# Norm products of q behind the tenth dense matmul, and the next batch's rows six positions apart

## Chip, cores and metric

The kernel runs on one core of one Trainium2 chip. Its time is the device time of that core in microseconds (us), from timed runs without a profiler; beside them stands one execution taken by the hardware profiler, whose records all views of the profile come from.

## What is computed

x is (4, 512, 512) in f32: four batches of 512 tokens, 512 wide. Three blocks follow one another, each on a layernorm of x:

```python
x = x + 0.5 * ffn(layernorm(x))
x = x + attention(layernorm(x))
x = x + 0.5 * ffn(layernorm(x))
```

The ffn is `down(silu(gate(x)) * up(x))` with 2048 inner columns; its weights are interpolated from control points. The attention, which is the stage of the change, is a gated delta rule with 16 key heads and 32 value heads of 128 columns (two value heads share one key head):

```python
q, k, v, z = split(x @ W_qkvz)                  # by key head
q, k, v = silu(causal_conv_of_4_taps(q, k, v))  # along the tokens
q = inv_scale**2 * rms_norm(q);  k = inv_scale * rms_norm(k)
beta = sigmoid(b);  g = -exp(A_log) * softplus(a + dt_bias)   # a, b from x @ W_ba
for each token t and value head:
    S = S * exp(g_t)
    delta = (v_t - k_t @ S) * beta_t
    S = S + outer(k_t, delta)
    o_t = q_t @ S
out = (rms_norm(o) * norm_w * silu(z)) @ W_out
```

## The kernel before

The tokens of a batch are cut into four chunks of 128, and the recurrence over tokens is done chunk by chunk as matmuls (f32), with the inverse of a triangular matrix for the part inside a chunk. The attention walks through 64 units, 4 batches of 16 key heads, in slots: `slot(un)` (L1533) holds the work of unit `un` and, beside it, that of its neighbours.

Of unit `un` itself: the projections of q and of the two v, each of four dense matmuls (`project`, L1033; the matmul is L1041, 128x128 weights against 512 columns, in the profile `pj` with w_q, w_v, w_k). Behind the fourth matmul of each come, by a calendar, the convolution (`taps`: one ScalarE step at L1049, three VectorE steps at L1051, all called acc), three positions later tanh on ScalarE (th, L1059) and one position later the silu on VectorE (L1063), which gives q or v. Of unit `un`+8 (`LEAD` is 8): the projection of its key (w_k), again four dense matmuls. Then 16 more dense matmuls: the gates z of this and the next unit in even slots (pz, L1359), the output projection of two finished units in odd ones (py, L1507). These 32 matmuls are the list `dense`.

Of unit `un`-1: the recurrence, eleven steps from `recur` (L1390) for its four chunks. `read_state` multiplies k and q with the state (pks, L1398), then VectorE makes rr (L1408) and, one position later, ScalarE tq (L1415). `solve` multiplies rr with the inverse (pzz, L1423), which ScalarE copies to zz (L1425). `write_state` multiplies zz with ks and pT (pos, L1434 and L1436), whence VectorE makes the new state (L1441, L1445) and, one position later, oo (L1451, L1455). Of unit `un`-2: the gating and turning of its outputs (`scale_outputs` L1485; `turn_o` with pgt, L1490, and gT, L1492).

The order is written out by hand. A slot goes through positions i = 0, 1, 2 and so on. At each it first does what the calendar has due (`later(d, f)` puts f d positions on), then the steps listed for this position by `after(i, step)`, then dense matmul i, so that position i lies behind i dense matmuls. The steps of the recurrence are put at the front of positions 1, 3, 5, 8, 10, 12, 16, 18, 20, 23 and 26: solve of the second chunk is at 8, its write_state at 10, read_state of the third at 12, its solve at 16. The instructions of TensorE, VectorE, ScalarE and GpSimd run in the order in which this code issues them; that of the DMAs on SyncE's queue is left to the compiler.

`norm` (L1244) is one of the steps of `after`. It takes the squared norms of q for the scaling of the RMS norm: `products` (L1067, the matmuls at L1072) does 16 small matmuls of 32x32 into a PSUM tile pqq; one position later `mean_square` (L1074) takes the diagonal on VectorE (dg, L1077), reduces and scales it (msq, L1079 and L1080) and has GpSimd take the root (rsq, L1082); three positions after that `roots` (L1254) makes rq and rqe, which the recurrence of this unit uses in the next slot. `norm` stands at position 9, together with `diagonal`, which works on the matrix to be inverted. `turn_k` (L1231; transposes of k, then ks on GpSimd) and `scores` (L1275; products k·k and k·q, pp) stand at 11 and 13. PSUM tiles come from three pools: pa with four banks (pj, pqq, py, pz, pp, pgt, pk, ln_pt and others share them in turn), pq and pi with two each.

Ten slots before a batch begins, in the slots un = 6, 22 and 38 (the "batch slots" for short), the rows of that batch are fetched and normalized by `begin` (L918), for t = 0 to 3: `load(t)` (L924) starts the DMA of 128 rows (L926) into xt, a tile with two buffers which it shares with osq, sp and et; three positions later `stats` (L931 to L936) takes mean and variance on VectorE and the root on GpSimd; one position later VectorE scales the rows (L938); `turn(t)` (L940), in the code of the slot `turn_x`, transposes them on TensorE into ln_pt (L945) and ScalarE copies that to xnT (L946). `load(t)` stands at position 7t and `turn_x(t)` at 7t + 6. In the slot that follows, the gates beta and g of the new batch are made (`log1p`, L979 to L998, on VectorE). Once a slot GpSimd multiplies out ee (`decay`, L1221), which has 1024 elements in each of 128 partitions.

Of the kernel before, what the change touches and what calls it, by code (L numbers as in the profile page):

```python
# [264 lines left out]
def tile_macaron(ctx, tc, x, w_qkvz, w_ba, conv_w, dt_bias, a_log, norm_w, w_out, cps, consts, grid, starts, out):  # L265
# [555 lines left out]
    def attention():  # L821


        with ExitStack() as st:
# [76 lines left out]
            def due():  # L901
                for f in calendar.pop(clock[0], ()):
                    f()
# [578 lines left out]
            def scale_outputs(s, r):  # L1482
                for t in range(NT):
                    u = 2 * t + r
                    nc.scalar.activation(s["oo"][:, t, r], s["oo"][:, t, r], AF.Copy, scale=s["orr"][:, u : u + 1])  # L1485

            def turn_o(s, r):
                po = bank(pa, "pgt", [P, NT, P])
                for t in range(NT):
                    nc.tensor.transpose(po[:, t, :], s["oo"][:, t, r, :], ident)  # L1490
                gr = w4.tile([P, NT, P], F32, name="gT")
                nc.scalar.activation(gr, po, AF.Copy, scale=nwh)  # L1492
                s["pair"].setdefault("gT", []).append(gr)

            def load_o(pair, n):
                pair["wo"] = w1.tile([P, 4, H], F32, name="w_o")
                nc.sync.dma_start(
                    pair["wo"], w_out[(n - 1) * 2 * DK : (n + 1) * 2 * DK, :].rearrange("(r p) h -> p r h", p=P)
                )

            def project_out(pair, xa):
                box = {}

                def step(t, r):
                    if r == 0:
                        box["py"] = bank(pa, "py", [P, H])
                    nc.tensor.matmul(box["py"], pair["gT"][r][:, t, :], pair["wo"][:, r, :], start=r == 0, stop=r == 3)  # L1507
                    if r == 3:
                        py = box["py"]
                        later(1, lambda: nc.vector.tensor_tensor(xa[:, t, :], py, xa[:, t, :], ALU.add))  # L1510

                return [lambda t=t, r=r: step(t, r) for t in range(NT) for r in range(4)]
# [7 lines left out]
            def keys_of(un):  # L1520
                b, n = units[un]

                def dd():
                    if un % GRP == 0:
                        diag[un // GRP] = w1.tile([P, 8 * GRP, BLK], F32, name="dd")
                    return diag[un // GRP]

                return keys(b, n, batches[b], heads[un], dd, un % GRP)
# [4 lines left out]
            def slot(un):  # L1533


                dense, at = [], {}

                def after(i, *steps):
                    at.setdefault(i, []).extend(steps)

                if un < N:
                    b, n = units[un]
                    pair = pairs.setdefault((b, n // 2), {})
                    p = prepare(un, b, n, batches[b], heads[un], inverse[un // GRP], un % GRP, pair)
                    if un == 0:
                        p["load"]()
                        p["load_z"]()
                        p["decay"]()
                        p["scan"]()
                    dense += p["dense"]  # L1550
                    after(11, p["turn_k"])
                    after(9, p["norm"], p["diagonal"])
                    after(11, lambda: p["scores"](0))
                    after(13, lambda: p["scores"](1))
                    after(17, p["join32_a"])
                    after(20, p["join32_b"])
                    after(21, lambda: p["turn_v"](0))
                    after(22, lambda: p["turn_v"](1))
                    after(23, lambda: p["join64"](0, None))
                    after(26, lambda: p["join64"](1, 0))  # L1560
                    after(29, lambda: p["join64"](None, 1))
                ku = un + LEAD
                if ku < N:
                    kk = keys_of(ku)
                    kk["load"]()
                    kk["decay"]()
                    dense += kk["dense"]
                    after(24, kk["blocks"])
                if un < N and n % 2 == 0:
                    dense += p["gates"]  # L1570
                if un >= 3 and units[un - 2][1] % 2:
                    b2, n2 = units[un - 2]
                    pair2 = pairs[b2, n2 // 2]
                    if n2 == 1:
                        xas[b2] = w1.tile([P, NT, H], F32, name="xa")
                        nc.sync.dma_start(xas[b2], x1[b2].rearrange("(t p) h -> p t h", p=P))
                    load_o(pair2, n2)
                    dense += project_out(pair2, xas[b2])
                if 2 <= un < N + 2:
                    last = un >= N  # L1580
                    after(0 if last else 2, lambda: scale_outputs(heads[un - 2], 0))
                    after(0 if last else 4, lambda: scale_outputs(heads[un - 2], 1))
                    after(0 if last else 6, lambda: turn_o(heads[un - 2], 0))
                    after(0 if last else 8, lambda: turn_o(heads[un - 2], 1))
                if 1 <= un < N + 1:
                    steps = recur(heads[un - 1], units[un - 1][1])
                    for i, f in zip((1, 3, 5, 8, 10, 12, 16, 18, 20, 23, 26), steps):
                        at.setdefault(i, []).insert(0, f)
                    after(22, lambda: square_sums(heads[un - 1], 0))
                    after(28, lambda: square_sums(heads[un - 1], 1))  # L1590
                    after(30, lambda: gate_outputs(heads[un - 1]))

                turn = un % GRP
                if turn == 0 and un + GRP < N:
                    running["inv"] = invert(diag[un // GRP + 1], inverse[un // GRP + 1])
                inv = running.get("inv") if un < N else None

                if un + LEAD + 2 < N and units[un + LEAD + 2][1] == 0:
                    b1 = units[un + LEAD + 2][0]
                    running["begin"] = begin(b1)  # L1600
                    batches[b1], load, turn_x, raw, sums = running["begin"]
                    for t in range(NT):
                        after(7 * t, lambda t=t: load(t))
                        after(7 * t + 6, lambda t=t: turn_x(t))
                if un + LEAD + 1 < N and units[un + LEAD + 1][1] == 0:
                    _, _, _, raw, sums = running["begin"]
                    after(3, raw)
                    after(24, sums)
                if un + 1 < N:
                    b1, n1 = units[un + 1]  # L1610

                    def loads():
                        q = prepare(un + 1, b1, n1, batches[b1], heads[un + 1], None, 0, pairs.setdefault((b1, n1 // 2), {}))
                        q["load"]()

                    after(13, loads)
                    for i, f in ((17, "decay"), (27, "scan")):
                        after(i, lambda f=f: prepare(un + 1, b1, n1, batches[b1], heads[un + 1], None, 0, pairs[b1, n1 // 2])[f]())
                    if n1 % 2 == 0:
                        after(31, lambda: prepare(un + 1, b1, n1, batches[b1], heads[un + 1], None, 0, pairs[b1, n1 // 2])["load_z"]())  # L1620
                for i in range(max(len(dense), max(at, default=0) + 1)):
                    due()
                    for f in at.get(i, ()):
                        f()
                    if i < len(dense):
                        dense[i]()
                    if inv is not None and i in PUMP:
                        next(inv, None)
                    clock[0] += 1
                if inv is not None and turn == GRP - 1:  # L1630
                    for _ in inv:
                        pass
                if un >= N:
                    drain()
                if 2 <= un < N + 2:
                    b2, n2 = units[un - 2]
                    if n2 == NK - 1:
                        due()
                        nc.sync.dma_start(x2[b2].rearrange("(t p) h -> p t h", p=P), xas[b2])
# [108 lines left out]
```

## Time and profile before

| what | value |
| --- | --- |
| timed runs, us | 3836.11, 3828.24, 3830.8; median 3830.8 |
| the profiled execution, its own time, us | 3776.52 |
| its span, first to last instruction, us | 3774.6 |
| granted TensorE clock, mean over the span (1.00 is full speed) | 0.974 |
| the 64 slots of the attention, roughly | 560 to 3340 us |
| busy in that stretch, us: TensorE | 2722.9 of 2780 |
| VectorE | 2156.8 |
| ScalarE | 1222.8 |
| GpSimd | 670.5 |
| share of the 16 DMA engines there | 0.21, 64 GB/s |
| granted TensorE clock there | 1.00 |

How to read it. PE is TensorE, PEld its loading of weights (which runs beside the matmuls), DVE VectorE, ACT ScalarE, POOL GpSimd, SP SyncE. L1041 is line 1041 of the kernel, `pj<-xnT,w_v` says which tiles an instruction writes and reads, x4 how many instructions a row gathers. In a timeline a row has its start (us from the start of the span), the time that the group took, engine, line and tile; in brackets stands how long the engine was idle before it and whose end it then waited for. The chain of work goes back from the last instruction of a window to what released each step; "issue" there is time in which nothing that the profile shows was waited for. In a table by windows each row has the window, its length, the busy time (and number of instructions) of PE, PEld, DVE, ACT and POOL, then the granted clock, the share of the DMA engines and their GB/s. The ends of matmuls are modelled in the records, so a busy TensorE need not be one at its peak. Before and behind the 64 slots lie the two ffn blocks and the start of the attention, which the change does not touch.

### The profile page before, as it was taken

What the parts mean: (1) busy time and instruction counts of PE and PEld (TensorE: products, weight loads), DVE (VectorE), ACT (ScalarE), POOL (GpSimd) and SP (SyncE); (2) the same over time, 40 slices, a digit from 0 to 9 for tenths busy, and PEclk for the clock granted to TensorE, in tenths of its full rate; (3) what the DMA queues carried; (4) which work ended last, traced back from release to release, by engine and by line L of the source; (5) the groups of instructions that cost most, each with busy time, mean ns of one, the idle gap of its engine ahead of it and who ended that gap; (6) DMA issues with size and microseconds to landing.
All of it is one profiled execution on the core that took longest, in us unless ns stands there. A gap on an engine that the chain in (4) does not pass through costs nothing.

```text
span 3774.6 us, 62529 instructions
## 1 busy us (share of the span) xinstructions
PE 3561.9 (94%) x24568; PEld 1967.6 (52%) x24568; DVE 2544.4 (67%) x5928; ACT 1471.3 (39%) x3440; POOL 867.2 (23%) x655
## 2 busy tenths in 40 slices
PE   5999679999999999999999999999999999987998
PEld 2333245555555555555555555555555555553333
DVE  5223687777777787777777777777778777552321
ACT  2322134444444444444444444444444444442221
POOL 2113112212222222222222222222222221210221
PEclk7999889999999999999999999999999999997999
DMA  4436311212222222122122222222221111203452
GB/s 140 158 129 189 107 46 53 69 56 64 65 73 59 82 65 73 53 65 63 60 59 82 60 71 61 60 65 69 66 82 60 63 51 51 70 18 109 152 199 90
DMA packets 303093, 302.25 MB, mean 80 GB/s; under 512 B 96880, under 2 KB 231312, under 8 KB 302224
## 3 DMA queue, kind: packets, MB, share of 16 engines
q1 hardware_dynamic: 292560, 264.70, 22.4%
q0 software_dynamic: 10240, 33.56, 2.9%
q8 instruction: 194, 3.18, 0.3%
q14 instruction: 99, 0.81, 0.1%
HBM read 247.60 MB, written 50.59 MB: 79 GB/s over the span
## 4 chain that ended last, share of the span: by engine, by line
PE 68%; DVE 15%; POOL 6%; ACT 5%; DMA 3%; issue 3%; SPq 0%; DVEq 0%; POOLq 0%; ACTq 0%
PE pj L1041 14%; PE py L1507 11%; PE pz L1359 9%; DVE acc L1051 4%; PE pks L1398 4%; PE y L492 3%; PE pp L1283 3%; PE pg L439 3%; PE pu L439 3%; POOL oo L1480 3%; PE pos L1436 2%; DVE ee L1227 2%; PE pu L1344 2%; PE pzz L1423 2%; POOL orr L1479 2%
## 5 line engine op out<-in xcount | busy, mean ns | idle before, releaser
L1051 DVE SCALAR_TENSOR_TENSOR acc<-pj,cw,acc 128x511 f32<-128x511 f32 (+2 forms) x768 | 574.6, 748 | 187.4 <-ACT acc L1049 169.2
L1041 PE MATMUL pj<-xnT,w_v 128*128 128x512 f32 x1024 | 520.6, 601 | 0.0
L1359 PE MATMUL pz<-w_z,xnT 128*128 128x512 f32 x1024 | 514.0, 614 | 0.0
L1507 PE MATMUL py<-w_o,gT 128*128 128x512 f32 x1024 | 511.0, 613 | 0.4
L448 DVE TENSOR_TENSOR ffn_it<-pu,ffn_sg 128x512 f32<-128x512 f32 x128 | 88.4, 691 | 364.8 <-PE pu L439 251.4
L1041 PE MATMUL pj<-xnT,w_q 128*128 128x512 f32 x512 | 256.5, 604 | 9.4 <-ACT ksq L1112 9.4
L1041 PE MATMUL pj<-xnT,w_k 128*128 128x512 f32 x512 | 246.3, 601 | 3.4 <-DVE acc L1051 3.2
L1415 ACT ACTIVATE tq<-pks,rqe 128x128 f32<-128x128 f32 x384 | 120.3, 364 | 330.7 <-DVE rq L1256 192.6
L1485 ACT ACTIVATE oo<-oo,orr 128x128 f32<-128x128 f32 x512 | 162.7, 390 | 206.2 <-POOL oo L1480 206.2
L1082 POOL TENSOR_TENSOR rsk<-msk,phalf 128x4 f32<-128x4 f32 x64 | 66.9, 1045 | 719.2 <-DVE msk L1080 712.1
L1049 ACT ACTIVATE acc<-pj,cw 128x512 f32<-128x512 f32 x256 | 175.3, 685 | 137.4 <-PE pj L1041 137.4
L1507 PEld LDWEIGHTS py<-w_o,gT 128*128 128x128 f32 x1024 | 170.8, 190 | 108.5 <-issue 97.4
L1359 PEld LDWEIGHTS pz<-w_z,xnT 128*128 128x128 f32 x1024 | 170.2, 191 | 101.4 <-issue 90.4
L1082 POOL TENSOR_TENSOR rsq<-msq,phalf 128x4 f32<-128x4 f32 x64 | 65.0, 1015 | 681.8 <-DVE msq L1080 669.1
L1059 ACT ACTIVATE th<-acc 128x512 f32<-128x512 f32 x256 | 161.7, 632 | 147.7 <-DVE acc L1051 143.6
L1041 PEld LDWEIGHTS pj<-xnT,w_v 128*128 128x128 f32 x1024 | 170.5, 191 | 71.0 <-issue 64.4
L1221 POOL TENSOR_TENSOR ee<-ident,w 128x1024 f32<-128x1024 f32 x64 | 141.4, 2209 | 225.6 <-DVE pT L1292 225.6
L458 POOL DMA_INDIRECT nat<-hid,idx x128 | 123.2, 963 | 300.1 <-PE y_pt L509 104.1
L1473 DVE TENSOR_REDUCE om<-osq 128x4 f32<-128x512 f32 x128 | 87.1, 681 | 154.1 <-ACT osq L1472 154.1
L1166 DVE TENSOR_TENSOR inv<-inv,inv_tmp 128x30 f32<-128x30 f32 (+14 forms) x480 | 169.1, 352 | 16.5
L1479 POOL TENSOR_TENSOR orr<-om,phalf 128x8 f32<-128x8 f32 x64 | 105.1, 1642 | 311.9 <-DVE om L1477 311.9
L1423 PEld LDWEIGHTS pzz<-rr,tt 128*128 128x128 f32 x768 | 115.0, 193 | 114.8 <-DVE rr L1408 49.5
(213 smaller groups left out, 6836.5 us busy)
## 6 DMA issues: line engine op xcount, KB each, us to landing
hid<-ffn_it SPq DMA_DIRECT2D x128, 256.0 KB, 2.1
w_v<-in_L_attn_W_qkvz SPq DMA_DIRECT2D x64, 512.0 KB, 3.5
w_z<-in_L_attn_W_qkvz SPq DMA_DIRECT2D x64, 512.0 KB, 4.7
ab<-decay_c SPq DMA_DIRECT2D x64, 512.0 KB, 3.6
w_o<-in_L_attn_W_out SPq DMA_DIRECT2D x32, 1024.0 KB, 5.5
w_k<-in_L_attn_W_qkvz SPq DMA_DIRECT2D x64, 256.0 KB, 2.8
w_q<-in_L_attn_W_qkvz SPq DMA_DIRECT2D x64, 256.0 KB, 3.3
ad<-decay_b SPq DMA_DIRECT2D x256, 32.0 KB, 2.3
```

The costliest lines, as they stand in the source:

```text
L439: nc.tensor.matmul(pm, wc[k // 2][:, m, at : at + P], ft[k // 2], start=True, stop=True)
L1041: nc.tensor.matmul(pj, w()[:, c, col : col + DK], xnT[:, c, :], start=c == 0, stop=c == NC - 1)
L1049: nc.scalar.activation(acc, pj, AF.Copy, scale=cw[:, ch, 3:4])
L1051: nc.vector.scalar_tensor_tensor(acc[:, d:], pj[:, : S - d], cw[:, ch, 3 - d : 4 - d], acc[:, d:], ALU.mult, ALU.add)
L1059: nc.scalar.activation(th, box["acc"], AF.Tanh)
L1166: nc.vector.tensor_tensor(ee[:, j + 1 :, :j], ee[:, j + 1 :, :j], tj, ALU.add)
L1359: nc.tensor.matmul(pz, xnT[:, c, t * P : (t + 1) * P], pair["wz"][:, c].rearrange("p j k -> p (j k)"), start=c == 0, stop=c == NC - 1,)
L1398: nc.tensor.matmul(pks[:, j].rearrange("p r v -> p (r v)"), m[:, tok], box["state"].rearrange("p r v -> p (r v)"), start=True, stop=True,)
L1423: nc.tensor.matmul(pzz[:, r], s["tT"][:, 2 * t + r], rr[:, r], start=True, stop=True)
L1479: nc.gpsimd.tensor_tensor(s["orr"], om, phalf, ALU.pow)
L1485: nc.scalar.activation(s["oo"][:, t, r], s["oo"][:, t, r], AF.Copy, scale=s["orr"][:, u : u + 1])
L1507: nc.tensor.matmul(box["py"], pair["gT"][r][:, t, :], pair["wo"][:, r, :], start=r == 0, stop=r == 3)
```

## The change

Two edits in `slot`. The squared norms of q are taken at position 10 and no longer at 9, which puts them behind the tenth dense matmul, and behind the step of the recurrence at that position, since those are put in front. `diagonal` stays at 9. All that `norm` puts on the calendar moves on by one position with it: dg, the reduction and GpSimd's root from 10 to 11, rq and rqe from 13 to 14. In the three batch slots the rows are loaded at positions 0, 6, 12, 18 in place of 0, 7, 14, 21 and turned at 5, 11, 17, 23 in place of 6, 13, 20, 27; statistics and scaling follow the loads, at 3, 9, 15, 21 and 4, 10, 16, 22. Nothing is added to the work or taken from it.

```diff
@@ in slot(un) @@
                     after(11, p["turn_k"])
-                    after(9, p["norm"], p["diagonal"])
+                    after(9, p["diagonal"])
+                    after(10, p["norm"])
                     after(11, lambda: p["scores"](0))
...
                     for t in range(NT):
-                        after(7 * t, lambda t=t: load(t))
-                        after(7 * t + 6, lambda t=t: turn_x(t))
+                        after(6 * t, lambda t=t: load(t))
+                        after(6 * t + 5, lambda t=t: turn_x(t))
```

From this edit on every line of the changed kernel has a number higher by one.

## The prediction

> **What bounds the kernel now.** I read the page first, then who waits for whom on TensorE in the attention stage, then the chain of work through one slot, then the timeline of that place, and last the granted clock where a batch changes.
>
> From the page:
>
> ```profile
> span 3774.6 us, 62529 instructions
> PE 3561.9 (94%) x24568; PEld 1967.6 (52%) x24568; DVE 2544.4 (67%) x5928; ACT 1471.3 (39%) x3440; POOL 867.2 (23%) x655
> ```
>
> TensorE is the bound, and a gain must come out of the time in which it does nothing. The waits of TensorE alone in 560 to 3340 us, which is nearly all of the 64 slots (us in total, times, longest):
>
> ```profile
> PE pqq L1072 <- DVE q L1063: 35.1, 47, 0.8
> PE pks L1398 <- DVE state L1441: 10.0, 6, 3.3
> PE pzz L1423 <- DVE rr L1408: 8.0, 10, 1.1
> ```
>
> The first is the step that is moved; the second belongs almost wholly to the three slots that load the next batch (3.06, 3.07 and 3.35 us). The chain of work in 1130 to 1139.5 us, an ordinary slot:
>
> ```profile
> 1132.23 1.73 PE pj L1041 x4
> 1133.96 0.04 issue
> 1134.00 0.63 ACT tq L1415 x2
> 1134.63 0.58 ACT gT L1492
> 1135.21 0.53 ACT th L1059
> 1135.73 0.02 issue
> 1135.76 0.70 DVE q L1063
> 1136.46 0.04 issue
> 1136.51 0.46 PE pqq L1072 x32
> ```
>
> For 2.5 us the path leaves TensorE: ScalarE works through its queue (tq, gT, th), VectorE makes q, and pqq starts 0.05 us after that. The timeline of TensorE there, and below the dots the same place two slots later:
>
> ```profile
> 1134.72 1.02 PE L1041 MATMUL pj<-xnT,w_v 128*128 128x512 f32 x2
> 1136.51 0.46 PE L1072 MATMUL pqq<-q 128*32 128x32 f32 x32 [0.76 <-DVE q L1063]
> 1136.89 1.13 PE L1041 MATMUL pj<-xnT,w_v 128*128 128x512 f32 x2
> 1137.86 0.61 PE L1434 MATMUL pos<-zz,ks 128*128 128x128 f32 x4
> ...
> 1224.89 1.02 PE L1041 MATMUL pj<-xnT,w_v 128*128 128x512 f32 x2
> 1225.93 0.46 PE L1072 MATMUL pqq<-q 128*32 128x32 f32 x32
> 1226.31 1.12 PE L1041 MATMUL pj<-xnT,w_v 128*128 128x512 f32 x2
> 1227.28 0.61 PE L1434 MATMUL pos<-zz,ks 128*128 128x128 f32 x4
> ```
>
> From pj to pos it is 3.14 us in the upper slot and 2.39 in the lower, where q came in time. Of 64 slots 45 have the wait of 0.76 us, three (the batch slots) 0.60, the first one 12.2, and 15 none.
>
> **Part one: norm one matmul later.** A dense matmul is two passes of 0.43 us, 0.86 together. In the upper slot the ninth ends at 1134.72 + 0.86 = 1135.58. After the change the tenth follows at once, to 1136.44. Next is no longer pqq: at position 10 the recurrence's write_state stands first, then norm. Its pos products (four short ones with ks, four with pT, 0.44 + 0.45 us) need zz, which ScalarE copies from 1136.18 to 1136.57, behind the same tq, gT, th and one acc. So the wait is not gone but changes its cause: zz can be used at about 1136.62, 0.18 us late. Weights that are loaded only at the release cost a little more: a pzz group that had to wait took 0.58 us to its successor (816.71 to 817.29), an unhindered one 0.44 (1224.01 to 1224.46 in the lower slot), so +0.14. The pos group ends near 1136.62 + 0.89 + 0.14 = 1137.65. Then pqq: changing to its narrow weights cost 0.17 us in the lower slot (1224.89 + 0.86 to 1225.93), its products 0.38, and the dense matmul behind them runs 0.10 longer (1.13 against 1.02). The eleventh dense matmul in effect starts at 1138.30. Before, it started at 1138.75. The gain is 0.45 us, 0.53 if the change of weights behind the short pos products is half as dear; I take 0.5.
>
> What could take it back further on in the slot? Behind pqq VectorE runs without idling from q on (1135.76), and the sum of its work is unchanged, only reordered: state and oo now come ahead of dg, the reduction and the scaling (0.28 + 0.29 + 0.17, about 0.7 us with their gaps). So the new state is ready 0.7 us earlier and the next pks has more room than its 1.16 us. rr of position 12 comes at the same time as before, 1145.55; its reader pzz stood at 1146.99 with weights wanted 0.43 earlier, so about 0.5 us remain after the shift. The third pks started 0.84 us after its state, where one that waits starts 0.145 after: 0.7 us of room, plus 0.39 that VectorE idled on TensorE before (acc at 1102.85) and gets back. None is used up by 0.5, though little is left. POOL's rsq and ks come about 0.9 us later; ks is read in the next slot, and roots, moved from position 13 to 14 with norm, finds rsq done. One wait is new. In the built program the first key matmul (position 12; past the last key head a gate or output matmul) takes over pqq's PSUM bank, and waits for dg. dg ends near 1140.5 and that matmul would start at about 1142.2: 1.5 us of room.
>
> The slots: 45 of the 0.76 kind, of which three follow a batch slot. There VectorE also makes the gates (L979 to L998) and TensorE already waits for rr at 830.61 and for state at 836.66, so what is gained at pqq is lost there. 42 x 0.5 = 21. The 15 slots without a wait gain about 0.1 (a switch to narrow weights in a better place): 1.5. In the first slot one dense matmul moves under the 12.2 us: 0.9.
>
> **Part two: rows every six positions.** Twelve loads, statistics, scalings and turns move, in three slots of 64. No work is added, and from load to statistics (three positions) and on to the scaling nothing changes; only the turn comes one position sooner after it. On SP's queue two row loads now stand ahead of w_v, which is used a slot later (issued at 768.60): nothing. The buffer of row t is that of row t-2, whose turn (6t-7) is ahead of the load at 6t. Row 0: scaled by 756.37, turned at 756.88 or later: no wait. Its copy by ScalarE (0.60 us at 761.21) leaves the place ahead of th, so q is 0.5 earlier in that slot. Row 1: its scaling ends at about 767.1, the turn would come at 766.6: 0.5 us of wait, in which state comes anyway. Row 3 falls where VectorE idles 4.4 us: nothing. Row 2 decides. Before, its scaling (780.17) ran into POOL's ee (779.90) and took 1.92 us, not 0.55; that pushed state, and pks waited 3.06 us. After, VectorE's statistics end near 775.5, POOL's root near 776.1, and ee starts at once behind it, so the scaling meets it again: done at 778.1, while TensorE wants the turn at 775.2 to 775.8. The wait moves from pks to the turn, about 2.5 us, and state (taps 2.31, ww 0.86, state 0.60 later) arrives at 781.8, when pks does too. Saved are about 0.6 us of wait and the turn's 0.44, already done: 1 us a slot.
>
> [...] The trace, window by window (the column ahead of the last two is the granted clock):
>
> ```profile
> 780.00:784.00 4.00, 1.15 (x3) 1.00 (x4) 3.94 (x8) 0.42 (x1) 1.80 (x1) 0.78 0.00 0
> 784.00:790.00 6.00, 6.00 (x63) 3.65 (x62) 3.01 (x9) 2.83 (x8) 0.00 (x0) 0.58 0.00 0
> ```
>
> So each batch slot also loses about 3 us at half clock (782.2 to 789.0). [...] I go by the row: the clock halves again, 1 us a slot, 3 in all. [...]
>
> **Sum.** 21 + 1.5 + 0.9 + 3 = 26.4 us. Against the profiled execution, 3776.5 us: 3750. The median of the timed runs, 3830.8, is 54 us above it, and no view shows where. If TensorE is slower there by that 1.4%, the 18 us from the previous slot's last pos product to pqq stretch by 0.25: the 0.76 becomes 0.51 and the wait for zz vanishes, so the gain per slot is still 0.5. Predicted median: 3830.8 - 26 = 3805.
>
> **Rivals.** (a) As worked out, 3805: 0.56. (b) More: zz holds nobody (its copy or the weight load is dearer in my sum than on the chip), so the whole 0.76 goes: 45 x 0.76 = 34, with the rest 39, 3792; or the batch slots keep full clock, 9 more, 3796. For it: waits of TensorE on zz are nearly absent now (0.3 us). Against: ScalarE's queue times leave no doubt that zz comes after 1136.44. 0.2. (c) VectorE sets the pitch: the 0.5 us of room behind pzz and pks is smaller than it looks, TensorE waits there, and some 8 us remain: 3823. For it: VectorE never idles from q to the key taps. Against: slots without the wait pass pzz and pks freely, 44.5 us long instead of 45.1. 0.19. (d) Slower: the key matmul waits for dg, which now stands behind state and oo. It decides once dg is over 1.5 + 0.5 us later than I have it. If state itself were held up by pos, dg and every key matmul would be; at 1 us net in 42 slots that is +42, 3870, and at 0.3 us, 3843. VectorE reaches state at about 1139.4, pos is done before 1138: against. 0.05. That the change does not do what it says is excluded by the built program: pqq stands behind pos in all slots that have one.
>
> **Chances and range.** This kernel's measurement can tell about 0.2%, 7.7 us, from no change. Faster: (a), (b) and half of (c), 0.86. Within: the rest of (c) and a little of (d), 0.10. Slower: 0.04. The range reaches from (b) to near (c): 3791 to 3821.
>
> **What would show it.** Right: pqq no longer waits for q (35 us to under 3), a new wait of pos on zz of 0.1 to 0.3 us in some 40 slots, pitch 44.6 us. In batch slots a wait of ln_pt on xt at position 17 and none of pks. Wrong: waits of 0.3 us or more at pzz or pks in ordinary slots (c), of pj on dg (d), or granted clock 1.00 through the batch slots (b).

## The result, and the profile after

Six timed runs of the changed kernel took 3793.68 to 3804.39 us, median 3798.49; six of the kernel before 3826.38 to 3836.11, median 3829.73. That is 31.2 us less, a ratio of 0.9917 (95% interval 0.9907 to 0.9927). The forecast was 3805, 26 us less.

The page of the changed kernel:

```profile
span 3799.6 us, 62583 instructions
PE 3568.7 (94%) x24568; PEld 1973.5 (52%) x24568; DVE 2537.5 (67%) x5928; ACT 1463.3 (39%) x3440; POOL 875.7 (23%) x655
```

Read alone, it says that the kernel became 25 us slower: the span of before is 3774.6. It is a trap. The profiled execution of before took 3776.52 us, 53 us under the timed median; this one took 3801.46 us and lies among its own timed runs. So the two spans can't be compared, and I compare stretches. From the first w_q matmul of the attention to the transposes of k in slot 63 it is 2878.02 us before and 2847.03 after: 31.0 us less, near the timed difference. (One profile of each kernel stands behind the 31.0, six timed runs behind the 31.2; that they agree so closely is partly luck, as the part on the half clock shows.) What lies ahead of it and behind it is 25.0 and 31.0 us longer in the profile after, nearly all in the two ffn blocks; the point-by-point section comes back to that.

TensorE's waits in 560 to 3340 us, the same view as before:

```profile
PE ln_pt L945 <- DVE xt L938: 10.2, 6, 3.0
PE pzz L1423 <- DVE rr L1408: 10.1, 10, 1.1
PE pks L1398 <- DVE state L1441: 3.0, 4, 2.5
```

The wait of pqq for q (35.1 us, 47 times) is gone from it. So are the three waits of pks for state in the batch slots (9.5 of the 10.0 us); the 3.0 us left are 0.16 three times and one wait of 2.54 at 578.29, which before had too (2.53 at 554.43, outside this window). In the batch slots stand six waits at the turns of the new batch's rows: 0.40 and 2.98 us in each. pzz waits 2.1 us longer, 0.93 in place of 0.21 us in each slot that follows a batch slot: what is gained at pqq is lost there, as predicted. No wait of pos for zz is listed.

TensorE at the place of the change, an ordinary slot (un = 14, the one that the prediction showed):

```profile
1153.83 1.88 PE L1041 MATMUL pj<-xnT,w_v 128*128 128x512 f32 x4
1155.72 0.71 PE L1434 MATMUL pos<-zz,ks 128*128 128x128 f32 x4
1156.27 0.61 PE L1436 MATMUL pos<-zz,pT 128*128 128x128 f32 x4
1156.81 0.46 PE L1072 MATMUL pqq<-q 128*32 128x32 f32 x32
1157.20 1.13 PE L1041 MATMUL pj<-xnT,w_v 128*128 128x512 f32 x2
```

The ninth and tenth dense matmul stand together (four passes), then pos, then pqq, no bracket with idle time anywhere. But look at the starts. Below are four unhindered passes of before, then ScalarE's zz and the weight loads of pos after the change, and last the first such load of before, for the pos at 1137.86:

```profile
1132.07 1.88 PE L1041 MATMUL pj<-xnT,w_v 128*128 128x512 f32 x4
1133.79 0.67 PE L1423 MATMUL pzz<-rr,tt 128*128 128x128 f32 x4
...
1155.28 0.39 ACT L1425 COPY zz<-pzz 128x256 f32<-128x256 f32 x1
1155.72 0.52 PEld L1434 LDWEIGHTS pos<-zz,ks 128*128 128x128 f32 x4 [0.84 <-ACT zz L1425]
...
1137.43 0.19 PEld L1434 LDWEIGHTS pos<-zz,ks 128*128 128x128 f32 x1 [0.24 <-ACT gT L1492]
```

The unhindered passes took 1.72 us to the next instruction (1132.07 to 1133.79), those ahead of pos 1.89. The 0.17 is the wait for zz, which is done at 1155.67. The waits of the matmuls don't list it, since it hides under the modelled end of the last pass (0.59 us, of which 0.43 counts); those of the weight loads (engine PEld) do. And pos itself took 0.55 to its successor, not 0.44: its first weights came with the release and not 0.43 us ahead of the matmul, as before. A wait that is shorter than a matmul's tail shows in the distance from start to start, or at the weight loads. Over 560 to 3340 us the loads waited, in the changed kernel and then in the one with the earlier zz, which comes below:

```profile
PEld pos L1434 <- ACT zz L1425: 41.9, 62, 0.8
PEld pos L1434 <- ACT zz L1425: 11.6, 45, 0.3
```

By slots, from the transposes of k in one to those in the next, change against before, in us (worked out from the starts of these transposes in the two traces):

| slots | forecast | measured |
| --- | --- | --- |
| 42 ordinary ones that waited for q | -21 | -23.3 (0.555 each) |
| those that did not wait | -1.5 | -0.9 (0.085 each, 11 that lie in no batch region) |
| the first slot | -0.9 | -1.1 |
| three batch regions (three slots each, from the batch slot's predecessor on) | -3 | -5.7 (-0.7, -2.5, -2.4) |
| sum | -26.4 | -31.0 |

### The profile page after: what moved, and what is told of

Read it like the earlier page. It is cut to its first block, busy times and chain, and to the rows that moved or that the text cites. A ratio compares the mean times of both kernels' runs of the same rounds, so it can differ in the third digit from the quotient of the medians.

```text
span 3799.6 us, 62583 instructions
## 1 busy us (share of the span) xinstructions
PE 3568.7 (94%) x24568; PEld 1973.5 (52%) x24568; DVE 2537.5 (67%) x5928; ACT 1463.3 (39%) x3440; POOL 875.7 (23%) x655
## 4 chain that ended last, share of the span: by engine, by line
PE 84%; DVE 8%; issue 3%; POOL 2%; ACT 2%; DMA 1%; SPq 1%; another core or an unknown queue 0%; DVEq 0%; POOLq 0%; ACTq 0%
PE pj L1041 20%; PE pz L1359 12%; PE py L1507 12%; PE pks L1398 4%; PE y L492 3%; PE pg L439 3%; PE pu L439 3%; PE pzz L1423 3%; PE pos L1436 3%; PE pp L1283 3%; PE pos L1434 2%; DVE acc L1051 2%; PE pu L1344 2%; PE pf L374 2%; PE pv L1269 1%
## 5 line engine op out<-in xcount | busy, mean ns | idle before, releaser
L1041 PE MATMUL pj<-xnT,w_v 128*128 128x512 f32 x1024 | 509.5, 600 | 0.0
L1082 POOL TENSOR_TENSOR rsq<-msq,phalf 128x4 f32<-128x4 f32 x64 | 93.2, 1457 | 748.4 <-DVE ws L1234 748.4
L458 POOL DMA_INDIRECT nat<-hid,idx x128 | 122.7, 958 | 336.6 <-PE y_pt L509 137.9
```

The costliest lines, as they stand in the source:

```text
L1041: nc.tensor.matmul(pj, w()[:, c, col : col + DK], xnT[:, c, :], start=c == 0, stop=c == NC - 1)
L1082: nc.gpsimd.tensor_tensor(rs, ms, phalf[:, :NT], ALU.pow)
```

## The experiments

Kernels of one group ran on one chip, and each is compared with runs of the kernel before on that chip: norm only, rows only, norm first and early decay in one group (before: 3776.1 us); the two kernels with later turns, the rows in idle places and the changed kernel once more in a second (3828.2); the two with the late copy in a third (3827.1). "The stretch" below is from the first w_q matmul to the transposes of k in slot 63; the expectations of the first two groups count from the first pqq to the last, and are answered in that measure. Timed gains and those of the stretch differ by up to 7.7 us either way, so causes are read from the stretch and its slots, and the timed ratio stands beside it.

**Each edit alone.** The first has only the move of norm, the second only the row edit:

```diff
-                    after(9, p["norm"], p["diagonal"])
+                    after(9, p["diagonal"])
+                    after(10, p["norm"])
```

> Only the move of q's norm products to position 10; the next batch's rows stay seven positions apart. From the first pqq to the last it was 2851.7 us before the change and 2822.5 after it. Theory (the norm move gives 0.55 us in each slot that waited for q, the row edit some 5.7 us in and around its three slots): about 2828 us, timed ratio to the kernel before 0.9932. Rival (the whole gain is the norm move, the row edit gives nothing): 2822 to 2824 us, ratio 0.992. In the three batch slots the theory has a wait of about 3 us of pks for state again, and half clock behind it.

Measured: 2825.2 us, ratio 0.9921 (0.9907 to 0.9934). Between the two theories' numbers, and no decision by the sum alone. By slots it is clearer: the ordinary slots have the pitch of the changed kernel to 0.02 us (44.61, 44.18, 44.69 against 44.62, 44.18, 44.71), and the batch regions gained 1.2, 1.3 and 0.4 us; pks waited 3.06, 3.06 and 3.35 us there, as before the change.

```diff
-                        after(7 * t, lambda t=t: load(t))
-                        after(7 * t + 6, lambda t=t: turn_x(t))
+                        after(6 * t, lambda t=t: load(t))
+                        after(6 * t + 5, lambda t=t: turn_x(t))
```

> Only the row edit (loads at 6t, turns at 6t + 5); q's norm products stay at position 9. Theory: all the waits of 0.76 us for q are back, and from the first pqq to the last it takes 2846 to 2849 us (2851.7 less 3 to 6): 2.5 to 3 us of wait at the turn of row 2 in place of 3.1 to 3.4 at pks, and a half-clock stretch behind it that is about half as long in some of the three slots. Timed ratio 0.9985 to 0.9993. Rival (the row edit is worth nothing by itself): 2851 to 2852 us, ratio 1.000.

Measured: 2845.4 us, ratio 0.9965 (0.9951 to 0.9978). This is just past the theory's upper end (6.3 us less, where 3 to 6 were expected). The timed median is 12.6 us below that of before, where 3 to 6 were expected too; the trace shows only half of it in the attention, and another 5.3 us of that profile lie ahead of it, which the edit doesn't touch. The batch regions gained 3.6, 0.9 and 2.4 us, and that spread is the half clock: with waits of 2.85, 2.84 and 2.84 us at row 2's turn, the clock was full behind the first, at half for 6.8 us behind the second and for 3.4 behind the third. From the first w_q on the two edits give 28.4 and 6.3 us against 31.0 together. With the time lost at half clock in the batch slots taken out (10.2 us before, 6.8 with norm alone, 5.1 with the rows alone, 6.8 with both) it is 25.0 and 1.2 against 27.6: the norm move is nearly all of it. (The loss is reckoned as half of the time at half clock; where this begins while TensorE still waits, it is up to 0.6 us smaller, which changes none of these sums by more than 0.2.)

**Is zz what is late now?** Norm products ahead of pos, at the same position:

```diff
-                    after(10, p["norm"])
...
+                if un < N:
+                    at.setdefault(10, []).insert(0, p["norm"])
```

> As the changed kernel, but at position 10 q's norm products stand ahead of the recurrence's pos products and not behind them. q is made some 0.24 us before the tenth dense matmul ends, so pqq should not wait, and zz gets 0.4 us of room where it now has none. Theory (zz decides by a hair: the first pos products take 0.71 us in place of 0.61 since their release comes just as they are due): the 0.10 us goes, but changing to narrow weights behind a dense matmul costs 0.17 us, so 0 to 0.1 us a slot, 2818 to 2823 us from the first pqq to the last. Rival (zz holds TensorE and the rest of the 0.76 us is still to be had): 0.2 us a slot less, about 2813 us.

Measured: 2807.4 us, ratio 0.9873 (0.9858 to 0.9889). My expectation of 0 to 0.1 us a slot is wrong, the rival's direction right: an ordinary slot is 0.28 us shorter still. TensorE there:

```profile
1123.02 1.88 PE L1041 MATMUL pj<-xnT,w_v 128*128 128x512 f32 x4
1124.83 0.46 PE L1072 MATMUL pqq<-q 128*32 128x32 f32 x32
1125.22 0.71 PE L1434 MATMUL pos<-zz,ks 128*128 128x128 f32 x4
1125.77 0.61 PE L1436 MATMUL pos<-zz,pT 128*128 128x128 f32 x4
1126.22 1.02 PE L1041 MATMUL pj<-xnT,w_v 128*128 128x512 f32 x2
```

From the first dense pass to the dense matmul behind both groups it is 3.20 us here and 3.37 in the changed kernel, and that matmul runs 0.11 shorter (1.02, not 1.13), since no narrow weights stand right ahead of it. I had read only the 0.71 against 0.61 and overlooked the 0.17 that the waits of the matmuls don't list.

But this edit changes two things, who waits for zz and the order of wide and narrow weights. So zz was made earlier without touching TensorE's order: of the two output copies gT that ScalarE does in this part of the slot, the first is issued behind zz.

```diff
-                nc.scalar.activation(gr, po, AF.Copy, scale=nwh)
+                if d:
+                    later(d, lambda: nc.scalar.activation(gr, po, AF.Copy, scale=nwh))
+                else:
+                    nc.scalar.activation(gr, po, AF.Copy, scale=nwh)
...
-                    after(0 if last else 6, lambda: turn_o(heads[un - 2], 0))
+                    after(0 if last else 6, lambda: turn_o(heads[un - 2], 0, 0 if last else 3))
```

> The changed kernel, but ScalarE's copy gT of the output turned at position 6 is issued three positions later, behind zz; the order on TensorE is untouched. Theory (in the changed kernel zz holds the pos products for 0.18 us, and their weights, loaded late, cost another 0.10; putting the norm products first gained just these 0.28): zz comes some 0.57 us earlier, so the same 0.28 us goes in 42 slots, 12 us; from the first w_q matmul to unit 63's transposes of k about 2835 us, against 2847.0 of the changed kernel and 2832.7 with the norm products first. Rival (putting them first gained by a cheaper order of wide and narrow weights): nothing changes, 2846 to 2848 us.

Measured: a stretch of 2832.6 us, ratio 0.9883 (0.9860 to 0.9906); an ordinary slot 0.28 us shorter than in the changed kernel, as with norm first. The four passes take 1.72 us to pos again and pos 0.45 to its successor, and its weight loads no longer wait over 0.3 us (the second of the two lines above). So it was zz, held by ScalarE's queue, and not the order of weights.

The same copy moved in the kernel before, with norm still at 9:

> The kernel before, with only that copy gT moved behind zz; q's norm products stay at position 9 and the rows seven apart. Theory (the wait for q is one of ScalarE's queue: tq, gT, th): th and q come 0.57 us earlier, 0.2 us of the 0.76 stays, and 42 slots gain 0.5 to 0.57 each, 21 to 24 us: from the first w_q matmul to unit 63's transposes about 2855 us, against 2878.0 before. Rival (another engine comes next right behind, VectorE for instance): less than 10 us, 2868 us or more.

Measured: a stretch of 2875.6 us, ratio 0.9993 (0.9983 to 1.0004): nothing in sum. That sum hides two parts. The slots outside the batch regions are 0.13 us longer each; the batch regions are 9.3 us shorter, and some 8.5 of this is half clock, which the profile of before had for 20.5 us in its batch slots and this one for 3.4. The theory failed; the number is within the rival's, but its cause is another. The chain of work at one slot:

```profile
1104.90 0.52 ACT th L1059
...
1105.99 0.26 ACT zz L1425
1106.26 0.60 ACT gT L1495
1106.86 0.04 issue
1106.90 0.46 PE pqq L1072 x32
```

th comes directly behind tq now, and q 0.57 us earlier, but pqq waits for gT: 41.6 us in 48 waits, where it had waited 35.1 for q. pqq doesn't read gT, so what it waits for is room. The traces don't number the banks; in the built program pqq used to take the PSUM bank of the first output transposes (pgt). With their copy put off, it gets the bank of the second, and the copy that frees that one comes behind zz. A wait of 0.75 us on data became one of 0.87 on a bank. In the changed kernel with the late copy pqq takes the same bank, but stands a matmul and two pos groups further back, and waits for nothing.

**Why does row 2's scaling take 2.1 us?** In the changed kernel, all engines at the first batch slot:

```profile
797.73 0.85 POOL L936 TENSOR_TENSOR at_rstd<-at_rstd,phalf 128x1 f32<-128x1 f32 x1 [3.57 <-DVE at_rstd L935]
798.55 1.89 POOL L1221 TENSOR_TENSOR ee<-ident,w 128x1024 f32<-128x1024 f32 x1
798.61 2.11 DVE L938 TENSOR_SCALAR xt<-xt,at_mv,at_rstd 128x512 f32<-128x512 f32 x1 [0.43 <-POOL at_rstd L936]
```

The root releases both, ee on GpSimd's queue and the scaling on VectorE, and they start within 0.06 us. The scaling ends 0.28 us behind ee, here as in the kernel before, where it started 0.26 us behind it. The next kernel issues ee ahead of the root:

```diff
-                    for i, f in ((17, "decay"), (27, "scan")):
+                    for i, f in ((14, "decay"), (27, "scan")):
```

> As the changed kernel, but GpSimd's multiplication ee for the next unit is issued at position 14 and not 17, so that in the three batch slots it stands ahead of row 2's root on GpSimd's queue and is over before row 2 is scaled. Theory (the scaling takes 2.1 us in place of 0.55 because it runs beside ee): the scaling is back at 0.55 us, the wait at row 2's turn falls from 2.98 to 1.5 to 2.2 us; if that escapes the half clock, 3 to 4.5 us a batch slot, 9 to 13 in all; if not, 1 to 1.5 a slot, 3 to 4.5 in all. From the first pqq to the last 2809 to 2819 us. Rival (the scaling is long for another reason, or the wait comes from elsewhere): the scaling stays at about 2 us and the stretch within 1 us of 2822.5.

Measured: 2816.2 us, ratio 0.9909 (0.9896 to 0.9923). Row 2 in the first batch slot:

```profile
771.51 1.90 POOL L1221 TENSOR_TENSOR ee<-ident,w 128x1024 f32<-128x1024 f32 x1 [2.56 <-DVE pT L1292]
773.36 0.99 POOL L936 TENSOR_TENSOR at_rstd<-at_rstd,phalf 128x1 f32<-128x1 f32 x1
774.38 0.55 DVE L938 TENSOR_SCALAR xt<-xt,at_mv,at_rstd 128x512 f32<-128x512 f32 x1 [0.43 <-POOL at_rstd L936]
```

The same instruction takes 0.55 us with ee over. The meeting was the cause. The turn's wait fell only to 2.41 us, since the root now queues behind ee for a microsecond; in two of the three slots the clock stayed full. ee meets another instruction in exchange: the silu vT (L1063), which runs beside it, takes 1.67 us and not 0.68, but is over before the root is.

**Where do the batch slots' waits end?** First with norm first, the early decay and the turns three positions later, then the turns alone on the changed kernel:

```diff
-                        after(6 * t + 5, lambda t=t: turn_x(t))
+                        after(6 * t + 8, lambda t=t: turn_x(t))
```

> Norm products ahead of pos (as in the run that put them first), ee issued at position 14 (as in the run with the early decay), and the rows' turns at 6t + 8 in place of 6t + 5. Theory: row 2's scaling takes 0.55 us and no turn waits for it any more; what is late is then the state, some 6.0 us behind the place where the turn used to be wanted, while pks wants it 4.5 us behind: a wait of 1.5 us in place of 2.98 + 0.40, and no half clock. From the first pqq to the last 2797 to 2800 us (2807.4 less 5.6, less the 3.4 us at half clock that that run had); timed ratio to the kernel before 0.984 to 0.986. Rival (VectorE's work in the batch slots sets their length wherever the turns are): waits in the batch slots still sum to about 3.4 us each, 2804 to 2808 us.

Measured: 2806.1 us, ratio 0.9898 (0.9882 to 0.9914). Its waits of TensorE:

```profile
PE pks L1398 <- DVE state L1441: 11.5, 7, 2.8
```

> As the changed kernel, only with the rows' turns at 6t + 8 in place of 6t + 5; ee still meets the scaling of row 2. Theory (the wait at the turn is TensorE arriving too early, but behind it VectorE is late anyway): the turns no longer wait, and pks waits some 2.2 us for state, so 0.8 + 0.4 us less in each batch slot; from the first pqq to the last about 2819 us, give or take what falls at half clock (0 to 3.4 us a slot). Rival (the turn's wait is the only one): 3.4 us less in each, 2812 us or lower.

Measured: 2824.8 us, ratio 0.9930 (0.9912 to 0.9949); pks waited 3.41 us for state in each batch slot. In both, the turns no longer wait and pks waits instead, 2.83 and 3.41 us. Both theories are wrong in size, by 1.2 to 1.3 us each time. The first one's rival is nearer: its stretch (2804 to 2808) came, though not its wait of 3.4 us. VectorE's work between positions 10 and 20 sets when these slots go on, wherever TensorE meets it.

So the rows' work has to leave that stretch. In ordinary slots VectorE idles some 2 us each at positions 3, 5 and 23. Loads and turns put by hand, with norm first and ee where it was:

```diff
-                        after(6 * t, lambda t=t: load(t))
-                        after(6 * t + 5, lambda t=t: turn_x(t))
+                        after((0, 1, 16, 18)[t], lambda t=t: load(t))
+                        after((7, 9, 21, 25)[t], lambda t=t: turn_x(t))
```

> Norm products ahead of pos, and the rows put where VectorE is idle in ordinary slots: loads at positions 0, 1, 16 and 18, turns at 7, 9, 21 and 25; ee at 17 as before. Row 2's statistics and scaling then come behind ee (positions 19 and 20) and behind the state of position 18. Theory: no meeting with ee, pks no longer waits for state; left are about 0.5 us at pzz (rr stands behind row 1's scaling) and up to 1 us at row 2's turn; no half clock. From the first pqq to the last 2796 to 2800 us, timed ratio 0.983 to 0.986. Rival (any place for the rows costs as much): waits of 3 us or more in each batch slot again, 2804 to 2808 us.

Measured: 2796.5 us, ratio 0.9855 (0.9834 to 0.9876), the shortest stretch of all (in timed runs its interval overlaps that of norm first): 56.1 us less than before, 19.3 of them in the batch regions, which had gained 8.3 with norm first and the rows six apart. Its waits of TensorE:

```profile
PE pzz L1423 <- DVE rr L1408: 11.0, 11, 1.1
...
PE pj L1041 <- ACT gT L1492: 1.1, 3, 0.4
```

No turn and no pks waits in a batch slot, 0.37 us of wait for a bank is all that is left there, and the clock stays full in all three.

**The half clock.** The changed kernel once more:

> The changed kernel once more, on the chip of the experiments. Theory: the slots outside the batch slots and the first one repeat to 0.05 us; the waits of 0.40 and 2.98 us at the turns too; only the time at half clock behind them differs, in steps of 1.7 us (0, 1.7 or 3.4 a slot), so from the first pqq to the last between 2815.7 and 2826. Timed ratio 0.9907 to 0.9927 as before. Rival (the half clock follows from the length of the wait): the same 3.4, 1.7 and 1.7 us again, 2822.5 us.

Measured: 2822.4 us, ratio 0.9928 (0.9914 to 0.9941). The waits in the batch slots are the same, 0.40 and 2.98 us. Eight microseconds behind each wait of 2.98, by windows (granted clock third from the right), first the changed kernel's first profile, then this one:

```profile
800.50:808.50 8.00, 7.63 (x22) 4.90 (x22) 5.49 (x12) 1.78 (x3) 0.00 (x0) 0.60 0.00 0
1527.50:1535.50 8.00, 7.74 (x72) 4.91 (x73) 6.75 (x16) 2.55 (x6) 0.00 (x0) 0.81 0.01 2
2253.00:2261.00 8.00, 7.95 (x72) 5.24 (x73) 6.42 (x15) 2.46 (x5) 0.00 (x0) 0.79 0.00 0
```

```profile
807.00:815.00 8.00, 7.68 (x72) 4.89 (x73) 6.76 (x16) 2.52 (x5) 0.00 (x0) 0.81 0.00 0
1532.30:1540.30 8.00, 7.71 (x71) 5.10 (x72) 6.46 (x15) 2.22 (x5) 0.00 (x0) 0.79 0.01 2
2257.80:2265.80 8.00, 7.63 (x22) 4.92 (x22) 5.50 (x12) 1.81 (x3) 0.00 (x0) 0.61 0.00 0
```

Same program, same waits, but the long half-clock stretch is behind the first wait in one profile and behind the third in the other. The regions differ accordingly: -0.7, -2.5, -2.4 us against before in the one, -2.3, -2.2, -1.2 in the other. The rival falls, though the sums happen to be alike. What differs is when the wait comes. In the traces of before and after all changes of the clock lie on one grid of 3413.3 ns, to within 3 ns (worked out from the traces' record of the clock), and in the batch slots of the experiments those that the windows show lie on such a grid to 0.01 us. The twelve waits of 2.98 or 2.99 us in the batch slots of four profiles (changed kernel twice, norm first, late copy) sort themselves by where they begin on it:

| begin of the wait behind a step of the grid, us | time at half clock, us |
| --- | --- |
| 0.31, 1.11, 1.13, 1.14 | 3.4 |
| 1.25, 1.32, 1.61 | 6.8 |
| 2.16 | none |
| 2.77, 2.78, 2.94, 3.21 | 3.4 |

The wait in the first batch slot of the changed kernel began at 1.25 in one profile and at 1.14 in the other. In these twelve waits of one length, then, the time at half clock goes with the place on the grid, and that is luck from run to run. Elsewhere the place did not tell it: of two waits of 2.83 and 2.84 us that both began at 1.42 (rows only; norm first, early decay and later turns) one was followed by 6.8 us and one by none.

## Why the prediction held, point by point

- **The stall of pqq** went, in all 48 slots that had it besides the first (11.5 us there); in the three behind the batch slots it came back at pzz, as forecast. Right.
- **The wait for zz takes its place**, 0.18 us plus 0.14 for weights loaded at the release. Measured 0.17 plus 0.11, and the experiment with the earlier zz gave exactly 0.28 a slot back. Right in cause and nearly in size. It is not among the waits of the matmuls, where I had said to look for it.
- **0.5 us a slot**: 0.555. The term for weights changing behind short products was the most mis-sized: I worked out 0.45 with it at 0.17 and 0.53 with half of it, and the trace has 0.10 between the last pos product and pqq. With this and the two terms of zz as measured the sum is 0.56. Over 42 slots the 0.055 above my 0.5 are 2.3 us of the 4.6 missed.
- **Nothing taken back further on**: in ordinary slots no wait of pzz, pks or a key matmul was added. dg ended at 1159.61 and the first key matmul started at 1161.22: 1.6 us of room, I had 1.5. (The 3870 and 3843 of rival (d) stand 27 us apart, where 42 slots at 1 and at 0.3 us make 29; nothing rests on it.) The rivals with VectorE as the pitch (c) and with dg (d) fall for these slots. That norm first gains another 0.28 there, all of it kept, shows that there was still more room.
- **The batch slots**: the wait moved from pks to row 2's turn, as forecast (2.5 us; measured 2.98), row 1 waited 0.40 (forecast 0.5), and the slow scaling came with it. The mis-sized term is the half clock: I let it be as long as before, three times 6.8 us, since in the trace of before waits of 2.53 and 2.36 us (up to 554.43 and 565.52) were followed by half clock too (0.50 in 554 to 560 us, 0.53 in 567 to 570), and it was 6.8, 3.4 and 3.4. That is 3.4 us of the 5.7, and it is luck rather than the edit: the repeated run had its long stretch elsewhere, and with norm alone, where pks waited as long as before, it was 3.4, 3.4 and 6.8 too. Without it the three regions gained 2.3 us, where I had 3.
- **Profile against median**: the forecast median was near, the forecast span (3750) not. I guessed that TensorE is 1.4% slower in the timed runs throughout. It is not: ordinary slots have the same length to 0.02 us in the group with the kernel before at 3776 us and in those at 3828 (norm first, 44.43 and 44.18 us in the one; 44.42 and 44.18 in the runs with the same order in the other). The 50 us lie in the two ffn blocks, where the later profiles have waits of TensorE without a named cause (31.0 us at pf, 16.8 at pg, 5.5 at y in the changed kernel) that the profile of before hasn't. During each of the long ones (5.5 to 14.0 us) GpSimd is gathering rows of the ffn (nat, L458), whose transfers took no longer than before (3.9 us from issue to the last packet, median, against 4.5). What they are stays open; no edit here touches them.

## What to carry to other kernels

When a stall is taken away by moving its step, ask what stands next in the queue of the engine that was late: here it was ScalarE, and zz, two instructions further on in it, became the new limit and kept 0.28 of the 0.84 us a slot that were to be had. Small waits hide in the tails of matmuls, as the 0.17 us for zz did here; measure from start to start, or look at the weight loads. Work that is inserted only now and then belongs where its engine idles in ordinary passes, which was worth more here (19.3 us against 8.3, norm first in both) than a spacing that only looks even; and ahead of moving a copy back, ask which later tile takes over the bank that it frees (0.87 us a slot here).

## What the runs showed of the hardware

Behind an idle stretch of TensorE in a batch slot the granted clock fell to a half for 3.4 or 6.8 us, or not at all, and the same wait gave all three. Of the twelve waits of 2.98 or 2.99 us one was followed by no half clock, eight by 3.4 us of it and three by 6.8. Of five between 2.35 and 2.41 us two were followed by 3.4 us and three by none; of six between 2.83 and 2.85 two by none; of five between 3.35 and 3.41 one by 3.4 and four by 6.8. The 3.4 and 6.8 us are one and two steps of the grid of 3.41 us. The shortest of these waits with half clock behind it was 2.35 us (the late copy in the kernel before), the longest without 2.98 (norm first).

The length of ee, too, goes with what VectorE does. In the traces of before and after it is 2.23 to 2.30 us in all 119 slots in which the silu vT is under way on VectorE when ee starts, and 1.89 to 1.97 in the nine others. In the batch slots of the kernel with the rows in idle places it was 2.23, in those of all the others 1.9. That vT itself is what ee meets was not tried.
